# Layer 1 of a four-layer kernel: thirteen single slots for x, z kept and normalised on chip, twelve a/b tiles, another order in the gate stage

## The chip, the cores and the metric

The kernel runs on one core of a Trainium2 chip. The metric is the device time of one execution in microseconds, as a median over several runs. The engines are PE (matrix products), DVE (vector), ACT (scalar functions), POOL (a second vector engine) and SP, which here only issues transfers. All four layers run in one launch, in float32.

## The reference, cut to what matters

The input is one image of 256 x 256 positions with 128 channels. Four residual layers follow each other; each normalises its input by channel groups first. The change is in layer 1, and in the first loads of layer 2:

```python
x = x + _L1_conv_ref(_gn(x), ...)
# with x now the normalised input of the layer:
a = sigmoid((x @ Wa1 + ba1) * (x @ Wa2 + ba2))      # 16 channels per position
b = sigmoid((x @ Wb1 + bb1) * (x @ Wb2 + bb2))      # 16 channels per position
g = sigmoid(x @ Wg + bg)                            # 128 channels
z = einsum('bikc,bkjc->bijc', a, b)                 # 16 products of 256 x 256 matrices
return g * (_ln(z, ln2_g, ln2_b) @ Wz + bz)         # _ln over the 16 channels
```

Layer 2 begins with the group normalisation of the result and, for each position, a mean and a variance over the 128 channels.

## The kernel before

Activations lie in DRAM with channels as rows (`x1T` is layer 1's input, `x2T` its result), and a tile is 128 channels by SC = 2048 positions, 1 MB; there are NSC = 32 of them. Layer 1 reads x twice, and has four stages. Each is under a manual schedule: each engine runs its instructions in the order in which the code issues them.

**Opening.** The order of the tiles, `order1`, alternates between the two halves of the image (0, 16, 1, 17, ...). `load1` (L775) fetches a tile into a pool: ten tiles (KEEP) in `x1_pool`, five more (MORE) in `xs_pool`. The first eight (FIRST) are issued ahead of a check on layer 0's result (L784 to L795): if numbers there are not finite, a slower path is taken; otherwise all engines branch past it. At that branch SP waits for the transfers which it has under way. Then the group normalisation of layer 1 is folded into its weights (L198 to L209, L818 to L829).

**The a/b stage (L853 to L875).** For each tile, sixteen matrix products make `p3_1` and `p3_2` (L859), ACT and DVE combine them (L868, L869), and one step later ACT takes the sigmoid into a `p3_ab` tile of 32 x 4 rows (`close3`, L842). `store3` (L848) writes it to `abD` in four parts, two on POOL's queue and two on SP's, another step later. There are five `p3_ab` tiles. Fifteen x tiles are asked for up front, and the later ones from step 10 on, five ahead. The first fifteen of the order are what the last stage starts with; the first ten stay where they are.

**The z stage (L877 to L942).** For each of the 16 channels (a plane), A is turned by PE (`tri_turn`, L1822), copied by ACT, and multiplied with B (`tri_multiply`, L1833). DVE subtracts plane 0 (L922), ACT squares (L924), DVE sums z (L928) and POOL sums the squares (L929). Each unscaled plane is stored to `znD` (L933). A and B come in pairs of planes (`load_z`, L898, L900), three pairs deep; five of the x tiles are fetched again between them. At the end the factor for each position is made in `s1` (L938 to L942).

**The gate stage (L948 to L1044).** For each x tile `gate4` makes the gate: four products of x with `wgf` (L982) into two PSUM tiles `p4_pg`, and ACT's sigmoid into `p4_g` (L985). `fetch_z` brings four tiles' worth of z into `p4_z` (L958); `scale_z` spreads `s1` over rows with sixteen small products (`p4_rb`, L969), and DVE multiplies (L972). Four products with `wz4` make `p4_pz` (L1014), DVE multiplies gate and product (L1022), POOL adds x (L1033) or, in every sixth step, DVE does (L1029). `sum4` lets ACT sum the squares of the tile before (L992), and SP stores it to `x2T` (L1039, L1044). A step's order is: gate two tiles ahead, z's scaling, z's product, DVE, POOL, `sum4`, store, load.

**Layer 2's beginning.** Statistics are finished (L1053 to L1072), seven tiles of x are loaded (`load5`, L1103), four are squared by ACT (L1108) and summed by PE (L1124).

Two things in the recorded program matter for what follows. Transfers on the hardware queues report to eight completion counters in turn, and an issuing engine waits for the earlier transfer of a counter before it uses it again, so SP has at most eight under way. And the first use of a tile in a newly opened pool waits for whatever last used that memory.

Of the kernel before, what the change touches and what calls it, by code (L numbers as in the profile page):

```python
# [9 lines left out]
F32 = mybir.dt.float32  # L10
AF = mybir.ActivationFunctionType
ALU = mybir.AluOpType
# [20 lines left out]
def kernel(ctx: ExitStack, tc: tile.TileContext, a: dict, out: bass.AP):  # L33
# [734 lines left out]

    order1 = [b + h * NSC // 2 for b in range(NSC // 2) for h in range(2)]
    KEEP, MORE, FIRST = 10, 5, 8  # L770
    x1_scope = ExitStack()
    x1_pool = x1_scope.enter_context(tc.tile_pool(name="x1", bufs=KEEP))
    xs = {}

    def load1(i, pool):  # L775
        s = order1[i]
        xs[s] = pool.tile([P, SC], F32, name=f"x1_{s}", tag="x1")
        nc.sync.dma_start(xs[s], x1T[:, s * SC : (s + 1) * SC])

    for i in range(FIRST):  # L780
        load1(i, x1_pool)
# [51 lines left out]
    with x1_scope, tc.tile_pool(name="xs1", bufs=MORE) as xs_pool:  # L833
        with tc.tile_pool(name="p3", bufs=3) as sb, tc.tile_pool(
# [4 lines left out]
            def close3():  # L839
                s, s1 = halves.pop(0)  # L840
                ab = sb.tile([P, CK], F32, name="p3_ab", bufs=5)
                nc.scalar.activation(ab, s1, AF.Sigmoid)  # L842
                done.append((s, ab))
# [8 lines left out]
            for i in range(FIRST, KEEP + MORE):  # L852
                load1(i, x1_pool if i < KEEP else xs_pool)  # L853
            for i, s in enumerate(order1):
# [8 lines left out]
                if i >= KEEP and i + MORE < NSC:  # L863
                    load1(i + MORE, xs_pool)
# [12 lines left out]
        with tc.tile_pool(name="zc", bufs=1) as zc:  # L877
            s1 = zc.tile([P, 2 * N], F32, name="z_s1")

            spread = zc.tile([P, 16, 32], F32, name="spread")  # L880
            for h in range(2):
                nc.gpsimd.tensor_copy(
                    spread[:, :, 16 * h : 16 * h + 16],
                    sel[:, 16 * h : 16 * h + 16].unsqueeze(2).to_broadcast([P, 16, 16]),
                )

            with tc.tile_pool(name="z", bufs=2) as sb, tc.tile_pool(
                name="zps", bufs=3, space=PSUM
            ) as ps, tc.manual_schedule():
                s2 = sb.tile([P, 2 * N], F32, name="z_s2", bufs=1)  # L890
                base = sb.tile([P, 2 * N], F32, name="z_base", bufs=1)
                AB, stores = {}, []

                def load_z(g):
                    if g < 8:
                        AB[g] = [sb.tile([P, 2, 2 * N], F32, name=n, bufs=3) for n in ("z_A", "z_B")]
                        A, B = AB[g]
                        nc.sync.dma_start(A, abD[2 * g : 2 * g + 2, :].rearrange("c (p t) -> p c t", p=P))  # L898
                        for c in range(2):
                            nc.sync.dma_start(  # L900
                                B[:, c, :], abD[16 + 2 * g + c, :].rearrange("(q s t) -> s q t", q=4, t=CK)
                            )

                def turn_z(k):
                    if k < 16:
                        return tri_turn(nc, ps, sb, AB[k // 2][0], k % 2, ident, nc.scalar.copy)

                for g in range(3):
                    load_z(g)
                at = turn_z(0)  # L910
                for k in range(16):
                    if k and k % 2 == 0:
                        load_z(k // 2 + 2)
                    nxt = turn_z(k + 1)
                    pz = tri_multiply(nc, ps, at, AB[k // 2][1], k % 2).rearrange("p t n -> p (t n)")
                    at = nxt
                    Z = sb.tile([P, 2 * N], F32, name="z_z", bufs=4)
                    if k == 0:
                        nc.vector.tensor_copy(base, pz)
                        nc.vector.memset(Z, 0.0)  # L920
                    else:
                        nc.vector.tensor_tensor(Z, pz, base, ALU.subtract)  # L922
                        sq = s2 if k == 1 else sb.tile([P, 2 * N], F32, name="z_sq", bufs=3)
                        nc.scalar.activation(sq, Z, AF.Square)  # L924
                        if k == 1:
                            nc.vector.tensor_copy(s1, Z)
                        else:
                            nc.vector.tensor_tensor(s1, s1, Z, ALU.add)  # L928
                            (nc.vector if k == 15 else nc.gpsimd).tensor_tensor(s2, s2, sq, ALU.add)  # L929
                    stores.append((k, Z))  # L930
                    if len(stores) > 1 or k == 15:
                        for k_, Z_ in stores if k == 15 else stores[:1]:
                            nc.sync.dma_start(znD[k_].rearrange("(p t) -> p t", p=P), Z_)  # L933
                        stores = stores[1:]
                    if k % 2 == 1 and KEEP + k // 2 < KEEP + MORE:
                        load1(KEEP + k // 2, xs_pool)

                nc.vector.scalar_tensor_tensor(s1, s1, -1.0 / 16, s1, ALU.mult, ALU.mult)  # L938
                nc.vector.tensor_tensor(s2, s2, s1, ALU.add)
                nc.vector.tensor_scalar(s2, s2, 0.0, None, ALU.max)  # L940
                nc.scalar.activation(s2, s2, AF.Sqrt, bias=epst, scale=1.0 / 16)
                nc.vector.reciprocal(s1, s2)  # L942
# [4 lines left out]
            with tc.tile_pool(name="p4", bufs=3) as sb, tc.tile_pool(  # L947
                name="p4psg", bufs=2, space=PSUM  # L948
            ) as psg, tc.tile_pool(name="p4psz", bufs=2, space=PSUM) as psz, tc.manual_schedule():
                zs, gts, sums = {}, {}, []  # L950
                junk = sb.tile([P, SC], F32, name="p4_junk", bufs=1)
                by_dve = (5, 11, 17, 23, 29, NSC - 1)

                def fetch_z(i):
                    if i < NSC:
                        zs[i] = sb.tile([P, 2, CK], F32, name="p4_z")
                        for m in range(2):
                            nc.sync.dma_start(  # L958
                                zs[i][:, m, :],
                                znD.rearrange("k (j b t) -> b j k t", j=8, t=CK)[order1[i] + m],  # L960
                            )

                def scale_z(i):
                    if i < NSC:
                        rb = psg.tile([P, 2, CK], F32, name="p4_rb", tag="p4_pg")
                        for m in range(2):
                            for c in range(4):
                                q = slice(32 * c, 32 * c + 32)
                                nc.tensor.matmul(  # L969
# [29 lines left out]
                for i in range(LEAD + 1):  # L999
                    gate4(i)  # L1000
# [874 lines left out]
```

## Time and profile before

| | |
|---|---|
| median of 6 runs | 3431.84 us (3427.98 to 3435.21) |
| the profiled execution | 3427.34 us, span 3425.6 us |
| PE, DVE, ACT, POOL busy, share of the span | 92%, 66%, 59%, 47% |
| mean granted TensorE clock | 0.957 |
| moved | 753.23 MB, mean 220 GB/s |

The stages of layer 1 in the profiled execution, by their first and last instruction: opening 1478.3 to 1505.4 us, a/b 1505.4 to 1595.5, z 1595.5 to 1649.5, from z to the first product of the gate stage 1649.5 to 1672.4, gate stage to DVE's last work 1672.4 to 1855.5.

A table by stage lists for each stretch its length, each engine's busy time with the number of instructions, the granted TensorE clock, the share of the time in which the DMA engines were busy, and what they moved. A row of the timeline is the start, the duration, the engine and line, the operation with output and inputs, the count, and in brackets how long the engine had been idle and what ended that. "SPq" rows are transfers being issued; a row that merges several lasts from the first issue to the last. A row of a group is busy time and mean ns, then idle time ahead of it by what ended it.

### The profile page before, as it was taken

The page shows a single profiled execution, that of the slowest core. Times are in us where ns is not written, and L with a number is a line of the kernel's source. Part 1 is how long each engine was busy: PE and PEld are TensorE (multiplying, and loading weights), DVE is VectorE, ACT ScalarE, POOL GpSimd, SP SyncE. Part 2 cuts the span into 40 slices and gives each one's busy share as a digit, 9 for nine tenths or more (in the row PEclk, how much of TensorE's full clock was granted, in tenths as well). Part 3 has the DMA queues.
Part 4 walks back from the last instruction along what each step waited for, and adds up shares of the span by engine and source line. Part 5 has one row for each costly group of instructions (what it writes and reads, how often), then busy time and mean ns, then how long its engine had stood idle before and what let it go on. Part 6 is the DMA issues. An engine that isn't in the chain of part 4 may idle for free. (4 is left out here: it accounts for less than half of the span.)

```text
span 3425.6 us, 52984 instructions
## 1 busy us (share of the span) xinstructions
PE 3135.3 (92%) x20394; PEld 1649.6 (48%) x20394; DVE 2263.3 (66%) x2612; ACT 2015.1 (59%) x2204; POOL 1617.1 (47%) x928
## 2 busy tenths in 40 slices
PE   6669999999999999956796999999999999859998
PEld 5425555555555555513332444444899533324444
DVE  5637888888888888832454445544555677747776
ACT  3667777777777777623576444443444466736565
POOL 4047777777777777723364000000555344514443
PEclk7889999999999999979998999999999999979999
DMA  9882333333333333279595676856999898856764
GB/s 393 349 303 86 108 120 107 119 110 120 107 118 115 111 119 107 98 278 369 195 379 243 241 267 255 309 212 237 341 353 348 306 337 334 307 163 194 206 201 130
DMA packets 298860, 753.23 MB, mean 220 GB/s; under 512 B 75193, under 2 KB 145819, under 8 KB 249067
## 3 DMA queue, kind: packets, MB, share of 16 engines
q1 hardware_dynamic: 290571, 741.54, 59.6%
q0 software_dynamic: 7520, 6.67, 0.6%
q8 instruction: 163, 2.67, 0.3%
q10 hardware_dynamic: 512, 1.59, 0.1%
q14 instruction: 94, 0.77, 0.1%
HBM read 462.02 MB, written 287.66 MB: 219 GB/s over the span
## 5 line engine op out<-in xcount | busy, mean ns | idle before, releaser
L564 DVE TENSOR_TENSOR p_e<-p_S,triT 128x1024 f32<-128x1024 f32 x512 | 609.1, 1211 | 144.3 <-PE p_S L554 144.3
L574 POOL TENSOR_TENSOR p_es<-p_e 128x1024 f32<-128x1024 f32 x256 | 603.4, 2369 | 124.2 <-issue 66.6
L572 ACT ACTIVATE p_e<-p_e,mbT 128x1024 f32<-128x1024 f32 x512 | 552.0, 1138 | 59.7 <-DVE p_e L564 59.5
L1167 PE MATMUL p_pm<-p_zn,wf 128*128 128x512 f32 x1040 | 451.5, 596 | 1.4 <-DVE p_zn L1184 1.4
L539 PE MATMUL p_mm<-p_xn,w 128*128 128x512 f32 x768 | 404.6, 610 | 0.3 <-DVE p_v L534 0.3
L1167 PEld LDWEIGHTS p_pm<-p_zn,wf 128*128 128x128 f32 x1040 | 198.0, 191 | 255.6 <-issue 248.8
L554 PE MATMUL p_S<-p_q,p_k 32*128 32x256 f32 x4096 | 294.9, 400 | 3.5 <-DVE p_e L564 3.2
L554 PEld LDWEIGHTS p_S<-p_q,p_k 32*128 32x128 f32 x4096 | 185.7, 184 | 159.4 <-PE p_mm L530 91.7
L1569 POOL TENSOR_TENSOR p_q<-p_q,p_pb 128x2024 f32<-128x2024 f32 x32 | 144.1, 4502 | 250.5 <-DVE p_pb L1563 250.5
L1233 POOL DMA_DIRECT2D rs__18031<-rs2D x4 | 2.0, 500 | 533.4 <-PE p_pm L1167 533.4
L1833 PE MATMUL tp_z<-p_B,tp_at 128*128 128x256 f32 x1024 | 251.0, 388 | 2.8 <-DMA p_B<-bD 2.5
L513 POOL TENSOR_TENSOR p_xn<-p_xn,p_rs 128x1024 f32<-128x1024 f32 x63 | 151.1, 2398 | 204.5 <-ACT p_xn L508 143.0
L587 PE MATMUL p_o<-p_e,p_v 128*32 128x256 f32 x4096 | 247.6, 382 | 0.0
L1276 POOL TENSOR_TENSOR k<-k,p_sq 128x512 f32<-128x512 f32 x128 | 163.0, 1273 | 135.5 <-ACT p_sq L1274 135.5
L1386 POOL TENSOR_TENSOR p_x<-p_x,p_g 128x2048 f32<-128x2048 f32 x30 | 136.2, 4542 | 161.3 <-DVE p_g L1373 117.5
L1833 PEld LDWEIGHTS tp_z<-p_B,tp_at 128*128 128x128 f32 x1024 | 185.6, 191 | 25.5 <-issue 2.8
L539 PEld LDWEIGHTS p_mm<-p_xn,w 128*128 128x128 f32 x768 | 125.6, 190 | 104.1 <-issue 87.9
L1275 DVE TENSOR_TENSOR k<-tp_z,k 128x512 f32<-128x512 f32 x128 | 88.6, 692 | 129.6 <-ACT p_sq L1274 129.6
L587 PEld LDWEIGHTS p_o<-p_e,p_v 128*32 128x32 f32 x4096 | 120.0, 109 | 109.2 <-ACT p_g L545 41.5
L1272 ACT COPY p_K<-tp_z 128x512 f32<-128x512 f32 x128 | 74.9, 585 | 160.2 <-PE tp_z L1833 160.2
L545 ACT ACTIVATE p_g<-p_mm,bgh 128x512 f32<-128x512 f32 x128 | 87.9, 687 | 131.4 <-PE p_mm L539 131.4
L1200 DVE SCALAR_TENSOR_TENSOR p_b<-p_pm,b2w,p_b 128x1024 f32<-128x1024 f32 x64 | 82.1, 1283 | 124.8 <-PE p_pm L1167 110.4
(374 smaller groups left out, 5977.6 us busy)
## 6 DMA issues: line engine op xcount, KB each, us to landing
p_x<-x2T SPq DMA_DIRECT2D x64, 1024.0 KB
x<-x1T SPq DMA_DIRECT2D x54, 1024.0 KB
p_x<-in_x_dram SPq DMA_DIRECT2D x32, 1024.0 KB
p_x<-xT SPq DMA_DIRECT2D x64, 512.0 KB
x2T<-x SPq DMA_DIRECT2D x32, 1024.0 KB
aD<-p_a SPq DMA_DIRECT2D x32, 1024.0 KB
bD<-p_b SPq DMA_DIRECT2D x32, 1024.0 KB
p_A<-aD SPq DMA_DIRECT2D x32, 1024.0 KB
```

Source lines behind the costliest of these rows:

```text
L513: nc.gpsimd.tensor_tensor(xn, xn, groups[g]["rs"], ALU.mult)
L539: nc.tensor.matmul(pm, lhsT=w, rhs=t["xn"][:, cs_], start=True, stop=True)
L554: nc.tensor.matmul(Ss[h // 2][:, h % 2, u, :], lhsT=t["k"][hp, r * N + u * P : r * N + (u + 1) * P], rhs=t["q"][hp, r * N : (r + 1) * N], ...
L564: nc.vector.tensor_tensor(e[:, :, 2 * p : 2 * p + 2, :].rearrange("p u h n -> p h u n"), Ss[p], triT[:, 2 * p : 2 * p + 2, :, :], ALU.add,)
L572: nc.scalar.activation(e[:, u, :, :], e[:, u, :, :], AF.Exp, bias=mbT[:, u, i : i + 1])
L574: nc.gpsimd.tensor_tensor(es, e[:, 0, :, :], e[:, 1, :, :], ALU.add)
L587: nc.tensor.matmul(t["o"][hp, r % 2, :], lhsT=t["v"][:, r * 2 + u, hp], rhs=e[:, u, h, :], start=(u == 0), stop=(u == 1),)
L1167: nc.tensor.matmul(pm[:, c, :], lhsT=wf2[:, i, :], rhs=zns[s][:, k * CK : (k + 1) * CK], start=True, stop=True)
L1276: nc.gpsimd.tensor_tensor(k2, k2, sq, ALU.add)
L1386: nc.gpsimd.tensor_tensor(xs7[s], xs7[s], gts[s], ALU.add)
L1569: nc.gpsimd.tensor_tensor(q[:, :, 1 : N - 2], q[:, :, 1 : N - 2], pb[:, :, 0 : N - 3], ALU.add)
L1833: nc.tensor.matmul(pz[:, t, :], lhsT=at[:, u, t * P : (t + 1) * P], rhs=Bc[:, u, :], start=(u == 0), stop=(u == 1))
```

## The change

- The two pools of x tiles become thirteen pools of one tile each, `slots`. A tile goes into a slot by its place in the order, in the a/b stage and in the gate stage, and the load of the tile thirteen places on follows when a slot's tile has been used. In the a/b stage this begins at step 0. What the gate stage starts with are the last thirteen tiles of the a/b stage, and its `order` is changed to suit: places 20 to 31 of `order1`, 19, 18, then 0 to 17. The z stage fetches no x.
- There are twelve `p3_ab` tiles.
- The planes stay in one tile `Z` of 32 KB a partition. When `s1` is known, DVE multiplies four planes at a time (L935 of the new kernel), and each four are stored to `znD` in one transfer. `scale_z`, its sixteen products, `spread` and the DVE product go.
- A and B of a pair share a tile in a pool `zg`. Its three tiles later hold gates 0, 1 and 2 of each seven; four other gate tiles lie in the gate stage's own pool.
- In the gate stage five gates are made ahead of the loop instead of three, z's product comes ahead of the gate, the gate is that of the tile four places on, and z is fetched three steps ahead into two tiles, not eight steps ahead into three.
- Layer 2's x tiles get a pool of their own, and its first four loads go on POOL's queue. In the recorded instruction order, three of these stand on POOL ahead of its last add, and SP's first stands ahead of the last two stores to `x2T`.

```diff
-    KEEP, MORE, FIRST = 10, 5, 8
-    x1_pool = x1_scope.enter_context(tc.tile_pool(name="x1", bufs=KEEP))
+    SLOTS, FIRST = 13, 8
+    slots = [x1_scope.enter_context(tc.tile_pool(name=f"x1_{i}", bufs=1)) for i in range(SLOTS)]
...
-                ab = sb.tile([P, CK], F32, name="p3_ab", bufs=5)
+                ab = sb.tile([P, CK], F32, name="p3_ab", bufs=12)
...
-                if i >= KEEP and i + MORE < NSC:
-                    load1(i + MORE, xs_pool)
+                if i + SLOTS < NSC:
+                    load1(order1[i + SLOTS], i % SLOTS)
...
+        gate_pool = x1_scope.enter_context(tc.tile_pool(name="zg", bufs=3))
...
+            Z = sb.tile([P, 16, 2 * N], F32, name="z_Z", bufs=1)
...
+                    ab = gate_pool.tile([P, 4, 2 * N], F32, name="z_ab", tag="g")
...
-                    if k % 2 == 1 and KEEP + k // 2 < KEEP + MORE:
-                        load1(KEEP + k // 2, xs_pool)
...
+            nc.vector.reciprocal(s1, s2)
+            for q in range(4):
+                zq = Z[:, 4 * q : 4 * q + 4, :]
+                nc.vector.tensor_tensor(zq, zq, s1.unsqueeze(1).to_broadcast([P, 4, 2 * N]), ALU.mult)
+                nc.sync.dma_start(znD[4 * q : 4 * q + 4, :].rearrange("c (p t) -> p c t", p=P), zq)
...
+            order = [order1[i] for i in (*range(20, NSC), 19, 18, *range(18))]
...
-                    zs[i] = sb.tile([P, 2, CK], F32, name="p4_z")
+                    zs[i] = sb.tile([P, 2, CK], F32, name="p4_z", bufs=2)
...
+                    gts[i] = (
+                        gate_pool.tile([P, SC], F32, name="p4_g", tag="g")
+                        if i % 7 < 3 else sb.tile([P, SC], F32, name="p4_g", bufs=4)
+                    )
...
-                LEAD = 2
+            LEAD = 4
...
-                    if i:
-                        gate4(i + LEAD)
-                    if i % 4 == 0:
-                        fetch_z(i + 8)
-                    if i % 4 == 2:
-                        scale_z(i + 2)
+                if i > 1 and i % 4 == 1:
+                    fetch_z(i + 3)
...
                     nc.tensor.matmul(
                         pz[c // 2][:, c % 2, :], lhsT=wz4[q, half, :], rhs=z[q, (i // 2) % 2, :],
                         start=True, stop=True,
                     )
+                if i:
+                    gate4(i + LEAD)
...
-                    j = i - 3 + KEEP + MORE
+                j = i - 3 + SLOTS
                 if i > 2 and j < NSC:
-                        load1(j, x1_pool if j % (KEEP + MORE) < KEEP else xs_pool)
+                    load1(order[j], (j + 7) % SLOTS)
...
-                xs[s] = sb.tile([P, SC], F32, name="p5_x", bufs=7)
-                nc.sync.dma_start(xs[s], x2T[:, s * SC : (s + 1) * SC])
+                xs[s] = x5_pool.tile([P, SC], F32, name="p5_x")
+                (nc.gpsimd if s < KB else nc.sync).dma_start(xs[s], x2T[:, s * SC : (s + 1) * SC])
```

## The prediction

> **What bounds the kernel now.** I read the page first: the span is 3425.6 us on one core, and layer 1 is its stretch from 1478 to 1861 us. Then the table by stage, which shows what each stage of the layer leans on, then the timeline at the joints, the groups of the two long stages, and the chain of waits at the end.
>
> ```profile
> core 0: us, PE busy (x) PEld busy (x) DVE busy (x) ACT busy (x) POOL busy (x), PEclk, DMA share, GB/s
> 1478.00:1505.00 27.00, 2.40 (x24) 2.25 (x24) 2.18 (x13) 1.54 (x2) 0.00 (x0) 0.50 0.84 332
> 1537.00:1595.00 58.00, 34.88 (x284) 8.63 (x276) 13.63 (x19) 22.71 (x38) 19.66 (x40) 0.95 0.97 388
> 1600.00:1650.00 50.00, 40.14 (x193) 33.61 (x192) 21.39 (x32) 17.56 (x31) 16.46 (x13) 0.94 0.87 331
> 1650.00:1672.00 22.00, 14.69 (x40) 5.43 (x38) 7.08 (x7) 10.12 (x10) 0.00 (x0) 0.84 0.24 83
> 1725.00:1775.00 50.00, 46.82 (x176) 16.71 (x175) 26.93 (x41) 36.73 (x37) 34.78 (x8) 1.00 0.99 379
> ```
>
> Rows in order: the opening loads, the a/b stage, the z stage, the step from z to the gates, the gate stage. All engines idle in the first, DMA is full in the second and third, all is slack in the fourth, and PE and DMA are both full in the fifth.
>
> ```profile
> 1478.31 24.63 SPq L778 DMA_DIRECT2D x<-x1T  x10
> 1487.06 0.56 PE L198 MATMUL gn_pm<-gn_mv,gmat 128*128 128x1 f32 x2 [7.84 <-PEq L795]
> 1502.14 0.16 DVE L202 TENSOR_TENSOR gn_d<-gn_mv,gn_mean 128x1 f32<-128x1 f32 x1 [14.33 <-SPq L795]
> ...
> 1653.63 3.35 DVE L942 RECIPROCAL z_s<-z_s 128x512 f32<-128x512 f32 x1 [0.79 <-ACT z_s L941]
> 1659.59 9.54 PE L982 MATMUL p_pg<-x,wgf 128*128 128x512 f32 x16 [6.30 <-ACT p_g L985]
> 1672.37 1.14 PE L1014 MATMUL p_pz<-p_z,wz 32*128 32x512 f32 x8 [1.39 <-issue]
> ```
>
> The layer's first eight loads issue at 1478.31; SP's branch (L795) lets go only when they have landed, at 1502.14. The gate stage proper begins at 1672.37.
>
> ```profile
> L842 ACT ACTIVATE p_ab<-p_s 128x512 f32<-128x512 f32 x32 | 20.1, 627 | 39.2 <-DMA abD<-p_ab 38.9 <-DVE p_s L869 0.3
> ...
> PE tp_a L1822 <- DMA z_A<-abD: 9.0, 4, 3.2
> ...
> L1033 POOL TENSOR_TENSOR x<-x,p_g 128x2048 f32<-128x2048 f32 x26 | 117.8, 4529 | 86.7 <-DVE p_g L1022 86.3
> L982 PE MATMUL p_pg<-x,wgf 128*128 128x512 f32 x232 | 107.3, 605 | 5.1 <-ACT p_g L985 5.1
> L969 PE MATMUL p_rb<-z_s,spread 32*32 32x512 f32 x112 | 14.2, 623 | 8.0 <-ACT p_g L985 8.0
> ...
> 1855.51 5.04 DMA x2T<-x
> 1862.13 12.01 DMA p_x<-x2T
> 1874.16 2.10 ACT p_sq L1108
> ```
>
> ACT waits 38.9 us for stores of a/b; the z stage waits four times for A; in the gate stage PE spends 14.2 us on the broadcast product `p_rb` and idles 8.0 + 5.1 us behind ACT. The last lines are the chain: the last x2T store takes 5.04 us, then layer 2's loads 12.01 us.
>
> **1. Opening loads.** The old pool's first load waits for layer 0's very end. In the new instruction list the first single slot waits only for the last `p_z` product (1459.97 + 0.64) and POOL's `p_es` (ends 1459.92): 1460.7, that is 17.6 us earlier. Later ones wait for completion counters shared with ACT's last row transfers (landed 1468.56), so all eight are out by about 1471. The eight took 1478.3 to 1502.1 = 23.8 us, so they land near 1484.5. Next late is PE's branch, 1487.06, whose input is pushed back while the loads share DMA with layer 0's last row and x1T transfers: 0 to 3 us, I take 2, as half a megabyte at half rate costs about that. L202 then runs near 1490: **12 us** (9 to 14).
>
> **2. The a/b stage.** Between 1521 and 1527 PE had stopped: five `p_ab` tiles, with their stores queued behind seven loads on SP, and new loads only from step 10, so DMA fell to 100–270 GB/s for some 11 us. Twelve tiles and a load at every step remove that. Volume is unchanged: after the opening, 24 loads and 8.4 MB of stores, at 421 GB/s (1.31 MB in the 3.11 us of a steady step). The last load should be in about 74 us after DMA resumes at 1503.5, or 10 us before the old 1587.8. But SP now lags: at that point some 13 steps of a/b stores are left, 26 issues of 0.37 us = 10 us and 2 to land, against about 7.7 us from there to the old first z load (1595.5). So **5 us** (0 to 8).
>
> **3. The z stage.** Five 1 MB loads of x and the 4 MB of unscaled z leave it; 8.4 MB of A and B remain. From 1606.65 to 1611.05 a plane takes 2.2 us with nothing late. First product 1601.57, the second 1604.5, the rest at 2.2: plane 15 starts at 1635.2, its subtraction ends 2.7 us later at 1637.9, against 1649.54. **12 us** (9 to 12): A of the fourth group is issued at 1606.6 and wanted 6.6 us later.
>
> **4. From z to gates, a loss.** Count from the last subtraction, E. The reciprocal ends at E+7.4 as now. New: DVE scales all planes in four instructions of 128x2048; nearest row 2.34 us (L1160), so to E+16.9. Then the last 1 MB store, nearest 5.04 us: E+22. Only then may z be fetched, and ACT write gates 3 and 4, whose tiles lie where Z lay. PE has waited since about E+16. The first product after the 6.30 us gap above came in 3.7 us for a half gate instead of 1.85. The Trainium skill (TensorE: Matmul & The Clock Gate, What's actually happening) says that an idle window of about 3.4 us halves the clock, and that speaks against this change: gate 4 costs 3.7 + 2.0 after ACT's 1.1, so first `p_pz` at E+29, without the rule E+27; today E+22.8. I take the trace's slow half: **−6 us** (−9 to −3).
>
> **5. The gate stage** took 1672.37 to 1855.48 = 183.1 us. Gone: `p_rb` 14.2 and its wait 8.0. Two more gates lie ahead of the loop: 2 × 3.70 = 7.4. With z's product ahead of the gate, PE meets ACT's sum one step later: that sum waits for POOL, 8.4 us after a `p_pz` (1696.85 to 1705.23), and must end, with a gate behind it, within two steps now and three then. At 4.7 us a step (1714.96 to 1719.66) the latter holds: 5 us. Sum 34.6. Against it DMA: steps 3 to 21 each load and store 1 MB, and every fourth fetches 0.5 MB of z, 2.23 MB a step. At 390 GB/s (8.9 MB in 22.83 us before) that is 5.7 us, at 421 it is 5.3; I take 5.5, above PE's 4.9 with the DVE steps. The z fetch has two tiles, not three, and is issued three steps ahead, behind 1 MB transfers in SP's order. For step 24 it is queued behind 18 steps of transfers that began at 18 us: 18 + 99 + 4.7 = 122 against 113. That costs 9 us: **25 us** (18 to 32). The x loads (51 instead of 54 in all, 19 instead of 17 here) and z stores (four instead of sixteen) are in these volumes.
>
> **6. End of the layer.** Now layer 2's first four loads go on POOL's queue and wait for the store of step 27, not for the last one; one more goes on SP ahead of the last two stores. POOL issues three ahead of its add for step 30, at 0.5 us each as with its other issues, while it had nothing to do. This could take the 12.01 us off the chain: four squares at 2.1 in place of it, about 6 us. A rule speaks against it: DMA: Bandwidth & Descriptors, Issuing engines are not separate DMA queues, says that all queues use the same 16 engines and interleave. The loads then share with the last four stores: 9.4 MB from 8 us before DVE's end, at 421 GB/s 22 us and 2 to land. The last store, for which the first square waits, lands 16 us after DVE's end instead of 5.04. Without the rule +6, with it −4. The 0.97–0.99 share in full stages sides with the rule; I take **−3 us** (−6 to +6).
>
> **The sum.** 12 + 5 + 12 − 6 + 25 − 3 = 45 us. The profiled execution, 3427.34 (its span is 3425.6), lies 4.5 under the median 3431.84; the gains are differences within it, so I set them against the median: **3387 us**.
>
> **Rivals.** *All of DMA's relief is real* (chance 0.15): the fetch is never late (+9), queues share better at the end (+8), a/b is 3 better: 65 us, 3367. For: 426 GB/s in the best stretches. Against: 99% share. *DMA takes most of the gate stage back* (0.17): at 6.2 us a step the fetch for step 24 lands at 135 rather than 122, 13 us, and step 1's early loads hold layer 0's tail by 5 more: 27 us, 3405. *The two-tile z fetch becomes the clock of the gate stage* (0.04): it is wanted 15.8 us after its issue. Six fetches must each be over 7.5 us late to eat 45 us, so it decides from 23.3 us per fetch; at 25 us the result is 10 slower, 3442. Against: backlog in SP's order is two steps, 11 us. *The slots do not release early* (0.06): without step 1 it is 33 us, 3399. The forecast keeps 0.58.
>
> **How the numbers follow.** The bounds sum to 21 and 69 us, but not all ends meet at once: 3371 to 3406 leaves out half of the first rival, little of the second and all of the slow one. About 0.2%, 7 us, is what measuring this kernel can tell from none. Faster 0.94; the same 0.02, the low tail of the second rival; slower 0.04, the third.
>
> **What would show it.** Right: L202 near 1490; no stop of PE in a/b before step 12; planes at 2.2 us throughout; four DVE products of about 2.35 us and 29 us from E to the first `p_pz`; no `p_rb`; PE waits on `p_z<-znD` late in the gate stage; a last x2T store of over 10 us with squares back to back behind it. Wrong: L202 still past 1500, z fetches late from the start, or PE in step with DMA at 5.7 us or more from step 3.

## The result, and the profile after

The changed kernel takes 3406.54 us (median of 16 runs, 3401.66 to 3414.01); the kernel before, run beside it, 3429.69 us (37 runs). The ratio is 0.993, with a 95% interval of 0.9917 to 0.9943, so the gain is 24 us, 20 to 28. The forecast was 45 us (3387): the sign was right, and the measured median lies half a microsecond above the top end of the range of 3371 to 3406.

The profiled execution has a span of 3401.2 us and a time of 3402.86. Cutting layer 1 at the same events in both traces gives this table, in us. The first column begins at POOL's last but one addition `p_u` (L626) in layer 0, which both kernels do in the same place.

| stretch of the trace | before | after | gain | forecast |
|---|---|---|---|---|
| layer 0's L626 to the first a/b product | 45.6 | 40.4 | 5.1 | 12 |
| from there to the first turn of z | 94.3 | 88.6 | 5.7 | 5 |
| from there to the last subtraction, E | 49.9 | 38.3 | 11.6 | 12 |
| E to the first `p_pz` | 22.8 | 29.3 | −6.5 | −6 |
| first `p_pz` to DVE's last gate product | 180.9 | 170.2 | 10.7 | 25 |
| from there to layer 2's first reciprocal | 26.9 | 30.2 | −3.2 | −3 |
| sum | 420.3 | 396.9 | 23.4 | 45 |

Four of the six steps came out within 1 us. Two fell short, by 7 and 14 us, and the experiments start with these.

The table by stage of the changed kernel, with the columns of the one shown before (each engine's busy time and count, then the granted TensorE clock, the DMA share and GB/s):

```profile
core 0: us, PE busy (x) PEld busy (x) DVE busy (x) ACT busy (x) POOL busy (x), PEclk, DMA share, GB/s
1477.00:1498.00 21.00, 5.74 (x27) 3.12 (x27) 5.80 (x22) 1.54 (x2) 1.86 (x1) 0.58 0.67 270
1530.00:1573.00 43.00, 28.85 (x246) 8.86 (x238) 11.64 (x16) 18.99 (x32) 15.32 (x32) 1.00 0.98 392
1589.00:1625.00 36.00, 35.85 (x186) 31.63 (x184) 19.90 (x30) 16.33 (x30) 15.64 (x13) 0.97 0.59 195
1626.00:1654.00 28.00, 18.30 (x39) 7.57 (x38) 15.23 (x10) 13.02 (x13) 0.00 (x0) 0.88 0.46 175
1700.00:1740.00 40.00, 37.68 (x128) 14.06 (x120) 22.24 (x34) 32.44 (x32) 30.59 (x8) 1.00 1.01 400
1740.00:1800.00 60.00, 49.19 (x150) 17.98 (x152) 27.01 (x40) 37.67 (x38) 32.72 (x8) 0.89 0.93 342
```

The z stage (third row) is now PE from end to end: 35.85 of 36 us, with DMA at 0.59 where it was 0.87. The gate stage (the last two rows) starts well, with DMA full and the clock at 1.00, and then falls off: from 1740 us PE works 49.19 of 60 us, at a clock of 0.89.

The timeline shows why the opening and the gate stage gave less. A row is start, duration, engine, line, operation, and in brackets the idle time before it and what ended it. First two rows of the kernel before:

```profile
1468.56 2.34 POOL L626 TENSOR_TENSOR p_u<-p_u,p_rb 128x1024 f32<-128x1024 f32 x1 [6.33 <-DMA p_rb<-rzD]
1478.39 0.17 DVE L788 TENSOR_SCALAR chk_ok<-gn_mv 128x2 f32<-128x2 f32 x1 [1.05 <-DMA x1T<-p_x]
```

The same and later moments in the changed kernel:

```profile
1459.14 35.94 SPq L778 DMA_DIRECT2D x<-x1T  x13
...
1476.52 2.34 POOL L626 TENSOR_TENSOR p_u<-p_u,p_rb 128x1024 f32<-128x1024 f32 x1 [15.87 <-DMA p_rb<-rzD]
...
1488.95 0.17 DVE L788 TENSOR_SCALAR chk_ok<-gn_mv 128x2 f32<-128x2 f32 x1 [3.79 <-DMA x1T<-p_x]
...
1495.59 0.16 DVE L202 TENSOR_TENSOR gn_d<-gn_mv,gn_mean 128x1 f32<-128x1 f32 x1
...
1634.27 8.90 DVE L935 TENSOR_TENSOR z_Z<-z_Z,z_s 128x2048 f32<-128x2048 f32 x4
...
1648.43 2.12 ACT L973 ACTIVATE p_g<-p_pg,bgf 128x1024 f32<-128x1024 f32 x2 [8.53 <-DMA znD<-z_Z]
...
1654.88 1.14 PE L997 MATMUL p_pz<-p_z,wz 32*128 32x512 f32 x8
...
1735.81 1.14 PE L997 MATMUL p_pz<-p_z,wz 32*128 32x512 f32 x8 [2.08 <-DMA p_z<-znD]
...
1761.92 2.09 PE L997 MATMUL p_pz<-p_z,wz 32*128 32x512 f32 x8 [5.81 <-DMA p_z<-znD]
...
1771.12 1.45 SPq L954 DMA_DIRECT2D p_z<-znD  x2
...
1787.30 2.20 PE L997 MATMUL p_pz<-p_z,wz 32*128 32x512 f32 x8 [4.75 <-DMA p_z<-znD]
...
1817.19 1.62 POOL L1088 DMA_DIRECT2D p_x<-x2T  x3
...
1842.70 8.05 ACT L1093 ACTIVATE p_sq<-p_x,mr2neg,gn_rstd 128x2048 f32<-128x2048 f32 x4 [10.79 <-DMA x2T<-x]
```

The x loads do leave 19 us earlier (1459.14, before 1478.31). But POOL now waits 15.87 us instead of 6.33 for layer 0's last row, and L788, the check on layer 0's result, comes at 1488.95 instead of 1478.39, although this execution is 1.6 us ahead at the start. So the branch is released by layer 0's late tail: L202 runs at 1495.59 without any idle time of its own, where it used to wait 14.33 us. The step from z to the gates is as foreseen: four DVE products of 2.2 us, gates 3 and 4 held until the last store of z has landed, 29.3 us from E. From its middle on, the gate stage lets PE wait for z three times; the fetch used at 1787.30 had been issued at 1771.12, 16 us before. At the end of the layer the first square waits for the last x2T store until 1842.70.

The groups (busy time, mean ns of one, then idle time ahead by what ended it) and, below them, a row of the waits (sum, times, longest):

```profile
L970 PE MATMUL p_pg<-x,wgf 128*128 128x512 f32 x256 | 123.7, 629 | 10.5 <-ACT p_g L973 9.7 <-DVE z_Z L917 0.8
...
L997 PE MATMUL p_pz<-p_z,wz 32*128 32x512 f32 x256 | 48.6, 703 | 19.3 <-DMA p_z<-znD 12.6 <-DVE p_g L1007 3.1 <-issue 2.6
...
L842 ACT ACTIVATE p_ab<-p_s 128x512 f32<-128x512 f32 x32 | 20.0, 625 | 24.2 <-DMA abD<-p_ab 23.9 <-DVE p_s L869 0.3
```

```profile
PE p_pz L997 <- DMA p_z<-znD: 12.6, 3, 5.8
```

`p_rb` of the gate stage and its wait are gone; PE's wait for z, 12.6 us in three pieces, has come instead. ACT's wait for a/b stores fell from 38.9 to 23.9 us.

### The profile page after: what moved, and what is told of

It is laid out like the page before. It is cut to its first block, busy times and chain, and to the rows that moved or that the text cites. A ratio compares the mean times of both kernels' runs of the same rounds, so it can differ in the third digit from the quotient of the medians.

```text
span 3401.2 us, 52669 instructions
## 1 busy us (share of the span) xinstructions
PE 3114.4 (92%) x20266; PEld 1652.8 (49%) x20266; DVE 2262.8 (67%) x2608; ACT 2014.8 (59%) x2204; POOL 1618.9 (48%) x930
## 4 chain that ended last, share of the span: by engine, by line
PE 38%; DMA 5%; POOL 2%; ACT 2%; issue 2%; DVE 1%; SPq 1%; ACTq 0%; POOLq 0%; DVEq 0%
PE p_pm L1152 13%; PE tp_z L1818 7%; PE p_pm L1305 6%; PE p_pm L1540 4%; POOL x L1018 2%; PE tp_a L1807 2%; PE p_st L1109 1%; DMA p_x<-x3T 1%; DMA p_t<-tD 1%; PE p_rz L1066 1%; PE p_pg L970 1%; PE p_pt L1577 1%; PE p_rk L1066 1%; DMA p_er<-eD 1%; PE p_eb L1066 1%
## 5 line engine op out<-in xcount | busy, mean ns | idle before, releaser
L554 PEld LDWEIGHTS p_S<-p_q,p_k 32*128 32x128 f32 x4096 | 185.7, 184 | 159.5 <-PE p_mm L530 91.7
L539 PEld LDWEIGHTS p_mm<-p_xn,w 128*128 128x128 f32 x768 | 125.7, 190 | 104.1 <-issue 88.2
L1260 DVE TENSOR_TENSOR k<-tp_z,k 128x512 f32<-128x512 f32 x128 | 88.6, 692 | 127.1 <-ACT p_sq L1259 127.1
L545 ACT ACTIVATE p_g<-p_mm,bgh 128x512 f32<-128x512 f32 x128 | 87.9, 687 | 131.3 <-PE p_mm L539 131.3
```

The lines of the kernel that those rows point to most:

```text
L539: nc.tensor.matmul(pm, lhsT=w, rhs=t["xn"][:, cs_], start=True, stop=True)
L554: nc.tensor.matmul(Ss[h // 2][:, h % 2, u, :], lhsT=t["k"][hp, r * N + u * P : r * N + (u + 1) * P], rhs=t["q"][hp, r * N : (r + 1) * N], ...
```

## The experiments

Each starts from the changed kernel unless the text says otherwise. The stretches are those of the table above, from one trace each; the ratio is to the kernel before, with its 95% interval. Stretches that an edit doesn't touch show the scatter of one trace: the a/b stage lay between 87.9 and 90.5 us, the z stage between 37.9 and 39.1.

| run | opening | a/b | z | to `p_pz` | gates | end | ratio |
|---|---|---|---|---|---|---|---|
| before | 45.6 | 94.3 | 49.9 | 22.8 | 180.9 | 26.9 | 1 |
| after | 40.4 | 88.6 | 38.3 | 29.3 | 170.2 | 30.2 | 0.993 [0.9917, 0.9943] |
| three early loads | 33.7 | 100.6 | 39.0 | 29.6 | 169.9 | 30.7 | 0.9955 [0.9939, 0.9971] |
| z fetched earlier | 40.3 | 87.9 | 38.1 | 31.8 | 158.8 | 31.2 | 0.9913 [0.9898, 0.9928] |
| z fetched by ACT | 39.7 | 89.6 | 37.9 | 29.1 | 167.0 | 31.7 | 0.9929 [0.9914, 0.9944] |
| layer 2's loads on SP | 40.0 | 88.2 | 38.2 | 29.3 | 168.2 | 23.7 | 0.99 [0.9883, 0.9916] |
| five a/b tiles | 40.2 | 90.5 | 38.4 | 29.4 | 170.1 | 30.3 | 0.9954 [0.9942, 0.9967] |
| earlier z and SP | 40.2 | 88.5 | 38.4 | 29.4 | 158.8 | 29.9 | 0.989 [0.9876, 0.9904] |
| the same, ten early loads | 43.9 | 89.3 | 39.1 | 30.0 | 159.3 | 29.5 | 0.9896 [0.9881, 0.991] |
| the same, POOL scales too | 41.3 | 88.9 | 38.8 | 33.3 | 159.5 | 30.4 | 0.9905 [0.9892, 0.9918] |
| the same, x moved in memory | 40.5 | 90.5 | 38.5 | 29.4 | 178.5 | 24.0 | 0.9932 [0.9918, 0.9947] |
| z stage with plane stores | 39.1 | 89.1 | 38.6 | 29.4 | 168.5 | 31.5 | 0.9928 [0.9916, 0.994] |
| z stage with x transfers | 40.6 | 88.6 | 42.7 | 30.7 | 169.8 | 32.7 | 0.9947 [0.9936, 0.9959] |
| before, twelve a/b tiles | 45.4 | 92.3 | 48.6 | 22.8 | 181.2 | 27.1 | 0.9995 [0.9987, 1.0003] |

**The opening: three early loads instead of eight.**

```diff
-    SLOTS, FIRST = 13, 8
+    SLOTS, FIRST = 13, 3
```

> Only the first three x loads of layer 1, not eight, are asked for ahead of the check on layer 0. Theory (the early megabyte loads share the DMA engines with layer 0's last row and x1T transfers and so hold its tail by about 10 us): POOL's wait at L626 for the row p_rb falls from 15.87 us to 6 to 10, L788's wait for the x1T store from 3.79 to about 1 to 2, and L202 comes at 1486 to 1490 instead of 1495.6; but five loads, 13 us of DMA time, move into the a/b stage, which grows by 6 to 12, so the whole is 0 to 6 us slower than the changed kernel. Rival (the tail is late for another reason, an order of instructions or a counter): L626 still waits 14 us or more and L202 stays within 2 us of 1495.6, so the whole is 6 to 12 us slower.

Rows of its timeline:

```profile
1476.16 2.34 POOL L626 TENSOR_TENSOR p_u<-p_u,p_rb 128x1024 f32<-128x1024 f32 x1 [11.38 <-DMA p_rb<-rzD]
...
1492.97 0.16 DVE L202 TENSOR_TENSOR gn_d<-gn_mv,gn_mean 128x1 f32<-128x1 f32 x1
```

The trace of this run stands 4.1 us later at L626 than that of the changed kernel, so 1492.97 answers to 1488.8, 6.7 us earlier. POOL's wait for the row fell from 15.87 to 11.38 us (6.33 with no early load), a little short of the 6 to 10 expected. Up to eight, the number of early loads sets the delay: no load, three, eight give 8.7, 13.7 and 18.2 us from the last but one L626 to the last (16.9 to 18.9 over the runs with eight). The early loads hold layer 0's tail. What they cost there they more than bring back in the a/b stage, which grew by 12 us without five of them; the whole is 8.6 us slower than the changed kernel by the two ratios, more than the theory's 0 to 6, though their intervals just touch.

**The gate stage: z fetched seven steps ahead into three tiles.**

```diff
-                    zs[i] = sb.tile([P, 2, CK], F32, name="p4_z", bufs=2)
+                    zs[i] = sb.tile([P, 2, CK], F32, name="p4_z", bufs=3)
...
+            fetch_z(8)
...
-                    fetch_z(i + 3)
+                    fetch_z(i + 7)
...
-            junk = sb.tile([P, SC], F32, name="p4_junk", bufs=1)
+            junk = sb.tile([P, SC], mybir.dt.bfloat16, name="p4_junk", bufs=1)
```

> The gate stage fetches z seven steps ahead into three tiles, as before the change, instead of three steps ahead into two (the throw-away output of the squares is bfloat16 to make room). Theory (the fetch comes late because it is asked for late, and each wait also costs a slow clock): PE's waits for p_z fall from 21 us in sum to under 4, L997's and L970's slow stretches go, and the gate stage shrinks from 172.3 to 154 to 162 us: the whole is 10 to 17 us faster than the changed kernel. Rival (DMA's pace of 5.74 us a step is the bound and the late fetch only its symptom): the waits move to x tiles or to slots that are not yet stored, the gate stage stays at 167 us or more, and the whole gains 5 us at most.

Its groups, and its row of the table by stage:

```profile
L970 PE MATMUL p_pg<-x,wgf 128*128 128x512 f32 x256 | 121.8, 621 | 17.3 <-ACT p_g L973 11.6 <-DMA x<-x1T 4.9 <-DVE z_Z L917 0.8
...
L998 PE MATMUL p_pz<-p_z,wz 32*128 32x512 f32 x256 | 47.3, 670 | 6.7 <-DVE p_g L1008 3.1 <-issue 2.6 <-PE p_pg L970 0.6
```

```profile
1740.00:1800.00 60.00, 54.68 (x177) 20.05 (x176) 33.08 (x50) 46.15 (x46) 43.85 (x11) 0.99 0.98 358
```

The wait for `p_z` is gone (12.6 us), and in the same stretch the clock is 0.99 instead of 0.89 and PE works 54.68 us instead of 49.19. The products themselves took 169.1 us (121.8 + 47.3) instead of 172.3. New are 4.9 us of waits for x. That makes 12.6 + 3.2 − 4.9 = 10.9 of the 11.4 us by which the stage shrank, to 158.8. So the theory holds for the cause. Of the rival there is only this: with z in time the DMA engines are busy for 0.98 of that stretch (0.90 of the whole stage), and for 4.9 us x is what comes late. The step to `p_pz` grew by 2.5 us, with gate 3 waiting 10.3 us for the stores of z instead of 8.5; the run with both repairs, which fetches z in the same way, does not repeat this (29.4). The whole gained 6 us by the ratios (their intervals overlap), and 8.8 in the sum of stretches, less than the theory's 10 to 17. (The 21 us of waits in this expectation and the next is an error: the trace has 12.6.)

**The same through ACT's queue, two tiles, three steps ahead.**

```diff
-                        nc.sync.dma_start(
+                        (nc.scalar if i > 4 else nc.sync).dma_start(
                             zs[i][:, m, :],
```

> z is fetched into two tiles and three steps ahead as in the changed kernel, but from the third fetch on through ACT's queue, past SP's queue of megabyte transfers. Theory (16 us from issue to use is the wait behind SP's megabyte transfers): issue to use falls under 9 us, PE's waits for p_z fall from 21 us to under 6, and the gate stage shrinks to 156 to 164 us, 8 to 15 us faster than the changed kernel. Rival (the DMA engines are the bound): issue to landing stays over 12 us or the x loads come later by the same amount, and the gate stage stays at 168 us or more.

Rows of its waits:

```profile
ACT p_g L973 <- DMA x<-x1T: 9.0, 2, 7.9
...
ACT p_g L973 <- DMA x2T<-x: 5.0, 1, 5.0
```

PE no longer waits for z, as expected, but the gate stage only comes down to 167.0. ACT now stands still for 14 us: by the recorded program each of these fetches waits, on ACT, for a completion counter that it shares with an x transfer of SP, and the sigmoids are queued behind. The wait moved from PE to ACT. How soon the fetches themselves landed no row shows.

**The end of the layer: layer 2's first loads on SP's queue.**

```diff
-                (nc.gpsimd if s < KB else nc.sync).dma_start(xs[s], x2T[:, s * SC : (s + 1) * SC])
+                nc.sync.dma_start(xs[s], x2T[:, s * SC : (s + 1) * SC])
```

> Layer 2's first four loads go through SP's queue again, behind the last stores. Theory (asked for early on POOL's queue they share the DMA engines with the last stores, on which the first square waits): the last store takes about 5 to 7 us, the loads about 12 behind it, and the stretch from DVE's end to the first square is 0 to 4 us shorter than the changed kernel's, so the whole is 0 to 4 us faster. Rival (the early loads do pay): the loads' 12 us stand on the chain behind the last store and the whole is 3 to 6 us slower than the changed kernel.

Its timeline:

```profile
1827.97 0.32 SPq L1029 DMA_DIRECT2D x2T<-x  x1
1828.33 4.24 SPq L1088 DMA_DIRECT2D p_x<-x2T  x5
1835.43 8.05 ACT L1093 ACTIVATE p_sq<-p_x,mr2neg,gn_rstd 128x2048 f32<-128x2048 f32 x4 [2.82 <-DMA x2T<-x]
```

The last store is issued at 1827.97 and the first square runs 7.5 us later; in the changed kernel it was 15.4 us (issue 1827.28, square 1842.70). The end stretch is 23.7 us, 6.5 less than in the changed kernel and 3.2 less than before. That is more than expected, since it beats the kernel before too: two of layer 2's loads were out ahead of the last two stores (1816.61 and 1818.89), the other five go behind, and the four squares ran in one piece (8.05 us). The whole is faster than the changed kernel, by 10 us by the ratios.

**The a/b stage: five tiles again, and twelve tiles in the kernel before.**

```diff
-                ab = sb.tile([P, CK], F32, name="p3_ab", bufs=12)
+                ab = sb.tile([P, CK], F32, name="p3_ab", bufs=5)
```

> The changed kernel with five p_ab tiles again instead of twelve, all else as changed. Theory (the a/b stage gained because ACT no longer waits for stores of a/b that are queued behind loads): ACT's wait at L842 for abD goes from 23.9 us back to 34 or more, PE stops again within the first dozen steps, and the stretch from the first a/b product to the first turn of z grows from 88.6 to 92 to 95 us: the whole is 3 to 6 us slower than the changed kernel. Rival (the load at every step is what filled the DMA engines and the tiles are idle reserve): the stretch stays under 90 us and the whole within 1.5 us.

The kernel before with that line the other way round:

> The kernel before with twelve p_ab tiles instead of five, and nothing else of the change. With five tiles in the changed kernel ACT still waited 35.7 us for stores but the DMA engines stayed full, so the load at every step filled them. Theory (either part alone keeps the DMA engines full: with twelve tiles PE reaches step 10, from which the kernel before loads, without its stop): ACT's wait for abD falls from 38.9 to under 28 us, the a/b stretch from 94.3 to 89 to 92 us, and the whole is 2 to 5 us faster than the kernel before. Rival (only the load at every step counts): the stretch stays at 93 us or more and the whole within 1.5 us.

The group L842, first with five tiles in the changed kernel, then with twelve in the kernel before:

```profile
L842 ACT ACTIVATE p_ab<-p_s 128x512 f32<-128x512 f32 x32 | 20.1, 628 | 36.2 <-DMA abD<-p_ab 35.7 <-DVE p_s L869 0.4
```

```profile
L842 ACT ACTIVATE p_ab<-p_s 128x512 f32<-128x512 f32 x32 | 19.9, 622 | 0.4 <-DVE p_s L869 0.4
```

The wait follows the tiles in both kernels, up from 23.9 to 35.7 us and down from 38.9 to nothing, but the stage hardly does: 90.5 instead of 88.6 (which another run reached without that edit), and 92.3 instead of 94.3. For the stage both theories expected more, and both rivals less, than was seen; about 2 us of the 5.7 can be the tiles', within the scatter. As a whole the first is 8 us slower by the ratios. Its profiled execution is 9.4 us longer than the changed kernel's: 2 of them lie in the stretches, and 5.0 ahead of the first stretch, in layer 0, which the edit doesn't touch (the L626 at which it begins stands at 1463.30, not at 1458.30). The second is not told apart from the kernel before. Since DMA stayed full with five tiles and a load at every step, the larger part goes to the load at every step, by subtraction. With twelve tiles alone DMA still fell off, from 15 to 30 us into the stage:

```profile
1530.00:1545.00 15.00, 14.55 (x138) 3.95 (x132) 6.75 (x9) 10.18 (x17) 9.07 (x20) 1.00 0.91 302
```

**The z stage: what had held it up.** First the planes 1 to 14 are stored again, one plane behind, to a spare place:

```diff
...
+                if k > 1:
+                    nc.sync.dma_start(znX[k - 1].rearrange("(p t) -> p t", p=P), Z[:, k - 1, :])
                 z = Z[:, k, :]
```

> The changed kernel, with each plane also stored unscaled to a spare place while the z stage runs, one plane behind, as the kernel before did (4 MB of extra stores). Theory (the z stage gained because SP's queue and the DMA engines no longer carry stores and x loads between the loads of A and B): with half of what was removed put back, PE's waits for z_ab return in part and the stretch from the first turn to the last subtraction grows from 38.3 to 42 to 46 us. Rival (the five x loads, a megabyte each, were what held up A and B; DMA at half its capacity has room for small stores): the stretch stays under 40 us.

Then five transfers of 1 MB instead (stores, where the kernel before had loads):

```diff
...
                     load_z(k // 2 + 3)
+                    if k // 2 < 5:
+                        nc.sync.dma_start(xX[:, (k // 2) * SC : (k // 2 + 1) * SC], xs[order1[20 + k // 2]])
```

> The changed kernel, with five transfers of 1 MB put back at the places in the z stage where the kernel before loaded x (here x tiles are stored to a spare place, since every slot is in use). Theory (SP's queue and the DMA engines no longer carry 9 MB of other transfers): with 5 MB of it put back the stretch from the first turn to the last subtraction grows from 38.3 to 42 to 48 us, with PE waiting for z_ab. Rival (the 4 MB of planes in sixteen stores, which wait in SP's queue for DVE, were what held up A and B): under 40 us.

A wait of PE in the second (its lines stand three lower), and one of SP in the kernel before:

```profile
PE tp_a L1810 <- DMA z_ab<-abD: 19.5, 4, 16.9
...
SPq L900 <- DMA x<-x1T: 7.6, 4, 2.0
```

The fourteen small stores change nothing: 38.6 us, the rival. The five large transfers bring three further waits for A and B, 19.5 − 16.9 = 2.6 us in sum (the longest is the one ahead of the first plane), and make it 42.7; PE is also busy for 1.8 us more, at a clock of 0.92 instead of 0.95. That is 4.5 of the 11.6 us. The other 7 were not reproduced; whether both kinds together, or the different order of the loads of A and B, made them stays open. One candidate: in the kernel before SP stood for 7.6 us at its loads of B until x transfers had landed, and in neither of these runs does it wait there.

**Both repairs together, and three attempts from there.**

> z fetched seven steps ahead into three tiles together with layer 2's first loads on SP's queue. Theory (the two losses are separate, in different stretches): they add: gate stage 157 to 161 us instead of 170.2 (from the first p_pz to DVE's last product), and from there to the end 9 us less, so 16 to 20 us faster than the changed kernel and a ratio of 0.987 to 0.989 to the kernel before. Rival (both give back the same DMA time at the end of the layer): only 10 to 12 us faster, 0.990.

Two rows of its table by stage:

```profile
1800.00:1814.00 14.00, 8.79 (x24) 2.66 (x24) 11.73 (x17) 7.95 (x8) 7.71 (x2) 0.64 0.42 149
1814.00:1830.00 16.00, 3.63 (x14) 1.73 (x14) 5.09 (x19) 5.73 (x6) 1.32 (x1) 0.50 1.00 405
```

They add only in part. The gate stage keeps its 158.8, but the end stretch is back at 29.9 (29.5 and 30.4 in the next two runs, which have the same two repairs). Over all stretches it gains 11.7 us on the changed kernel where the two alone gained 8.8 and 9.2; by the ratios it is 14 where they gained 6 and 10. DMA is busy for less than half of the time just before the end (0.42) and full after it (1.00). By the recorded program a load of layer 2 stands on SP, waiting for the store of step 27, with two later stores behind it: the timeline has that load at 1810.41 and the stores at 1810.78, though the second of the two tiles was complete by 1807.1. Still it has the lowest ratio, 0.989, and is ahead of the kernel before and, by intervals that no longer meet, of the changed one. It is not told apart from the run with SP alone (0.99).

Ten early loads on top of it:

> The same as e6_both, with ten x loads instead of eight ahead of the check on layer 0. Theory (the DMA engines lie idle for some 5 us between the landing of the eight loads and the first a/b products, and are full before and after): two loads of 2.5 us fill that gap, so the a/b stage shrinks by 4 to 5 us while the opening grows by 0 to 2: 2 to 5 us faster than e6_both. Rival (more early loads hold layer 0's tail further, 1.3 us a load as between three and eight, and SP's branch waits for them to land): the opening grows by 3 us or more, and the whole is no faster than e6_both.

The opening grew by 3.7 us and the a/b stage gave nothing back: the rival. Layer 0's last row, though, came no later than with eight loads, 18.0 us after the addition before it. The tenth load was issued only at 1495.31, when the row had been used (1480.51). Later by 2.6 us was the check at L788.

POOL takes the last four planes of the scaling:

```diff
-            for q in range(4):
+            for q in (0, 1, 3, 2):
...
-                nc.vector.tensor_tensor(zq, zq, s1.unsqueeze(1).to_broadcast([P, 4, 2 * N]), ALU.mult)
+                (nc.gpsimd if q == 3 else nc.vector).tensor_tensor(zq, zq, s1.unsqueeze(1).to_broadcast([P, 4, 2 * N]), ALU.mult)
```

> The same as e6_both, but POOL normalises the last four planes of z while DVE does the other twelve. Theory (DVE's four products of 2.2 us lie on the path from the last subtraction E to the first product of the gate stage): the last store leaves about 2 us earlier and the first p_pz comes at about E+29.5 instead of E+31.8; the whole 1.5 to 2.5 us faster than e6_both. Rival (the stores, 1 MB each, are what it waits for, or the two engines slow each other): E to p_pz changes by less than 0.7 us.

```profile
1642.11 6.63 POOL L935 TENSOR_TENSOR z_Z<-z_Z,z_s 128x2048 f32<-128x2048 f32 x1 [8.38 <-DVE z_s L932]
...
1644.27 6.61 DVE L935 TENSOR_TENSOR z_Z<-z_Z,z_s 128x2048 f32<-128x2048 f32 x1
...
1650.81 2.28 DVE L935 TENSOR_TENSOR z_Z<-z_Z,z_s 128x2048 f32<-128x2048 f32 x1
```

DVE's three products took from 1642.06 to 1653.08, 11.02 us, where four had taken 8.90. The first ended at 1644.3, the last took 2.28, but the middle one took 6.61 us: it ended 2.1 us after POOL's (1642.11 + 6.63 = 1648.74), as if it had begun only then. POOL's own product, 4.5 us long in the gate stage, took 2.1 more, about the length of DVE's first. So the two engines took turns. The Trainium skill (Trainium Architecture — The Big Picture, What this means for kernel authors) says that DVE and POOL share a pair of ports under an exclusive lock and not as a split of bandwidth. This trace fits that: 2.2 + 4.5 + 2.2 + 2.2 = 11.1. The attempt cost 3.9 us, 29.4 to 33.3. (The expectation's base of 31.8 was that of the run with the earlier fetch alone.)

Layer 2's x tiles are moved up in memory:

```diff
...
+        x5pad.tile([P, 2 * SC], F32, name="x5_pad")
```

> The same as e6_both, with layer 2's x tiles moved up by two tiles in memory, so that in SP's order the first of its loads stands behind three more stores of x2T than it did. Theory (e6_both gives back at the layer's end because SP stands before a load of layer 2 while finished stores of x2T are queued behind it, 3.9 us with DMA at 0.42 of its time): the first square comes 9 to 12 us after DVE's last product, not 15.9, and the whole is 3 to 6 us faster than e6_both. Rival (the DMA engines have a backlog there in any case): the first square stays at 15 us or more and the whole within 1.5 us.

```profile
POOL k L1235 <- DMA x2T<-x: 27.0, 1, 27.0
...
DVE k L1234 <- DMA x2T<-x: 23.4, 1, 23.4
```

The theory held where it was made: the first square came 9.5 us after DVE's last product, and the end stretch fell to 24.0. But the same move of memory let two clearings of layer 2's `k` tiles slip into the middle of the gate stage, one on DVE and one on POOL, where both engines then waited over 20 us for x2T stores. The gate stage grew by 19.7 us and the gain was lost.

## Why the prediction was right and where it was not

**1. Opening loads, 12 forecast, 5 measured: the term that failed is the delay of layer 0's tail.** It was put at 2 us for half a megabyte at half rate. The row alone came 9.5 us later (18.2 less 8.7), and L788 some 12 us (1488.95 against 1478.39, the trace being 1.6 us ahead). The loads landed early, though somewhat later than forecast (the DMA engines fall idle only at about 1486), but that no longer decided anything. The run with three loads shows the cause. With ten the row is no later still, but the check is, and the opening is longer.

**2. The a/b stage, 5 and 5.7.** PE's stop in the first dozen steps is gone, as predicted: it works for the first 41 us of the stage in one piece. The working named tiles and loads together; the runs give most to the loads, in part by subtraction.

**3. The z stage, 12 and 11.6.** Planes at 2.2 us with nothing late, as predicted. Which of the removed transfers had cost the time, the runs show for 4.5 us only.

**4. From z to the gates, −6 and −6.5.** First `p_pz` at E + 29.3 against E + 29, and the slow clock is there: gate 4's products took 5.35 us where a gate takes 3.70. Small misses cancel: half of gate 0's sigmoid went ahead of the square root on ACT, which put a table load of 1.28 us (ACT fetching another function) behind it, so the reciprocal ended at E + 8.7 and not at E + 7.4; DVE's products and gate 4 were each about half a microsecond shorter than reckoned.

**5. The gate stage, 25 and 10.7: two terms of the sum failed.** The late z fetch was put at 9 us. It cost 11.4 (170.2 less 158.8), and in three waits, not in one. The latency from issue to landing was taken as 4.7 us; from issue to use these three took 14 to 17, since SP's order puts each fetch behind megabytes under way. And the slow clock after a wait, 2.09 and 2.20 us for a `p_pz` of 1.14, was left out, though the very rule was weighed in step 4.

The larger error is in the 34.6 us of PE's savings: with z in time the stage still takes 158.8, a gain of 22. The groups of the stage alone, first in the kernel before, then with z fetched earlier:

```profile
L1014 PE MATMUL p_pz<-p_z,wz 32*128 32x512 f32 x256 | 44.1, 682 | 5.7 <-issue 5.2 <-PE p_pg L982 0.4
```

```profile
L970 PE MATMUL p_pg<-x,wgf 128*128 128x512 f32 x217 | 102.1, 613 | 5.1 <-DMA x<-x1T 4.9 <-ACT p_g L973 0.2
```

The savings that were named came nearly whole: `p_rb` and its wait (14.2 + 8.0), 5.2 us of gate products (107.3 to 102.1), 4.9 us of waits for ACT (5.1 to 0.2), 32.3 us together. Not in the sum were costs on PE that the kernel before did not have: 3.1 us of waits for DVE, 3.2 us more for z's products (44.1 to 47.3; after a step in which DVE adds, they stop between their halves and take 2.30 us), and 4.9 us of waits for x. That leaves 21 of the 22 us.

In that run DMA held PE up for no more than the waits for x and a slower clock around them. With both repairs PE was full for most of the stage, and DMA too:

```profile
1680.00:1700.00 20.00, 19.76 (x68) 7.11 (x64) 12.26 (x18) 16.36 (x16) 13.34 (x4) 1.00 1.00 405
...
1740.00:1760.00 20.00, 19.75 (x68) 7.34 (x64) 12.26 (x18) 16.28 (x17) 13.38 (x4) 1.00 0.97 343
```

The x loads went at 5.74 us a step (18 from 1673.80 to 1777.22), not at 5.5. An estimate from these traces: 19 loads and 31 stores of 1.05 MB and 4.2 MB of z are 56.7 MB, at 400 GB/s 142 us, and the first store leaves 8 us into the stage, so about 150. PE's own busy time with z fetched earlier is 146. So further savings on PE alone would soon have met DMA; no run tests this. That PE would be in step with DMA from step 3 was named as a sign of failure; it was not seen, since steps 3 to 14 went at 5.0 us on average, 4.7 apart from those next to DVE's additions, and the first wait for z came at step 16.

**6. End of the layer, −3 and −3.2.** The Trainium skill's rule in DMA: Bandwidth & Descriptors (Issuing engines are not separate DMA queues), that all queues interleave on the same 16 engines, decided rightly: the first square came 17.7 us after DVE's last gate product, which is 15.4 after DVE's last work, where 16 had been reckoned. The run with these loads on SP shows it from the other side, 9.7 us.

Of the rivals, that in which DMA takes most of the gate stage back came nearest, 3405, and for its reasons: early loads that hold layer 0's tail, and a z fetch that is late by 13 us (12.6 measured). Its pace of 6.2 us a step was too slow, and PE's new waits were not among its reasons, so part of the agreement is luck.

## What to carry to other kernels

Price an earlier transfer by what it delays as well as by what it brings: small transfers that something waits for, issued beside megabytes, took about 10 us longer here, on the same queue or on another. Before adding up what an engine saves, ask what its new order will make it wait for, and ask the DMA volume of the stage for its floor. Fetch a small tile as many steps ahead as there are large transfers queued in front of it. A repair that lets an engine finish sooner can be given back at the next joint, in an instruction order that no line of the edit shows, so read that order again after every change of memory.

## What the runs showed of the hardware that had not been expected

- Layer 0's last row came 1 to 2 us later for every megabyte load asked for ahead of it, up to eight: 8.7, 13.7 and 18.2 us with none, three and eight, but 18.0 with ten.
- A pair of z fetches of 0.25 MB each took 14 to 17 us from issue to use, where it was waited for, behind megabyte transfers of the same queue; on ACT's queue the wait was for shared completion counters, 14 us in sum.
- DVE and POOL, both multiplying 128x2048 in on-chip memory, took turns: a DVE product that takes 2.2 us alone took 6.61.
